# Three exact bf16 pieces for gathered tables and attention scores, block ends spread over more steps, and some products held back, in a four-layer graph network

## The chip, the cores and the metric

One core of a Trainium2 chip. The metric is device microseconds from the first to the last instruction of one execution. Every kernel below was run several times beside the kernel before on the same chip. Three chips were used for the experiments: one for e1 to e4, a second for e5 to e11, and a third for e12 to e14. On the first two the kernel before takes the same 2288 us; the third is slower, so its runs are kept apart.

## The reference, cut to what matters

There are 3327 nodes with 512 features and a sparse random adjacency matrix. Four layers follow each other, each with a residual and a layer norm. Layers 0 and 3 are graph attention (8 and 4 heads), layers 1 and 2 are means over neighbours.

```python
# layers 0 and 3
e    = leaky_relu(f_src[:, :, None] + f_dst[:, None, :])
attn = softmax(where(adj > 0, e, NEG_INF))
h    = elu(einsum('hnm,hmo->hno', attn, Wh))
# layer 1
agg = mask @ x / max(deg, 1)
out = relu(concat([x @ W_self + b_self, agg @ W_nb + b_nb]) @ W_comb + b_comb)
# layer 2: mean over the first 64 neighbours only
xj, xi = leaky_relu(nb_mean @ W_nb.T + b_nb), leaky_relu(X @ W_line.T + b_line)
# around each layer
x = layernorm(x + layer(x))
```

## The kernel before: the parts that matter

Rows are handled in 26 blocks of 128. The edges of a block come in chunks of 128. For each chunk POOL issues an indirect DMA (a gather) that fetches 128 table rows; DVE builds a 128 x 128 selection matrix; PE multiplies it with the rows and accumulates the block's sum. When a block's last chunk is done, a "block end" follows: residual, layer norm and the products that the next layer needs. The first seven blocks have 42 down to 10 chunks and are called heavy here; the other 19 have 9 down to 5, mostly 6 or 7, and are called light. "Moments" are a row's mean and variance, from which the layer norm is made.

Everything is written as generators. `Stages` advances each live one by one step per round, so a `yield` decides which instructions of other blocks come in between. In layers 1 to 3 each engine executes strictly in this program order; in layer 0 a scheduler chooses it.

```python
def step(self):
    for stages in list(self.live):
        if next(stages, self) is self:
            self.live.remove(stages)
...
def mean_group(item, table, near, gp, sp, pacc, accs, done):   # layers 1 and 2
    b, l, c0, g, at = item
    G = gather(gp, table, l, c0, g, D)                         # fp32 rows of 2 KB
    yield
    S = select(sp, ..., c0, g)
    yield
    for c in range(g):
        nc.tensor.matmul(accs[b], S[:, c, :], G[:, c, :], start=..., stop=...)
...
# attention scores (layers 0 and 3), fp32
nc.tensor.matmul(pe[:, c], ds[:, c*P:(c+1)*P], self.fall[:, H:, b], start=True, stop=True)
...
def summed(self, fin, acc, xb):          # block end of layers 0 and 3
    for s in range(2):                   # two halves of the heads
        nc.vector.tensor_scalar(rden[:, s], acc[s][..., OUT:OUT+1], 1e-30, None, ALU.max)
        nc.vector.reciprocal(rden[:, s], rden[:, s])
        nc.vector.tensor_mul(h[:, s], acc[s][..., :OUT], rden[:, s].to_broadcast(...))
    nc.vector.tensor_scalar(e, hq, 0.0, None, ALU.min)
    nc.scalar.activation(e, e, AF.Exp)
    nc.vector.scalar_tensor_tensor(hq, hq, 0.0, xb, ALU.max, ALU.add)
    yield
    nc.vector.tensor_add(e, e, hq)
    mv, rs = moments(fin, e)             # DVE statistics, then POOL computes rs = 1/std
    yield
    return e, mv, rs
...
def layer1_end(b, acc):
    yield
    ...                                  # y = relu(acc / deg + zb) + xb
    mv, rs = moments(fin, y)
    yield
    scaled(x2, y, mv, rs)                # DVE
    xt = transposed(fin, ps, x2)         # PE, then ACT
    yield
    nc.vector.tensor_add(tb, times(ps, xt, wn2), bn)
    store(t2_d, b, tb, 2)
    yield
    nc.vector.tensor_add(xi, times(ps, xt, wl2), bl)   # the "own" product
    nc.vector.scalar_tensor_tensor(xi, xi, SAGE_ALPHA, xi, ALU.mult, ALU.max)
    nc.vector.tensor_add(xres[b], xi, x2)
```

Of the kernel before, what the change touches and what calls it, by code (L numbers as in the profile page):

```python
# [8 lines left out]
F32 = mybir.dt.float32  # L9
# [522 lines left out]
GROUP = 4  # L532
SPAN = 10
RANGE = 60.0


class EdgeList:


    def __init__(self, pool, name, cuts, L, K, rounds, at):  # L540
        self.cuts, self.L, self.K, self.rounds, self.at = cuts, L, K, rounds, at
        self.idx = pool.tile([P, L], U32, name=f"idx{name}")
        self.dst = pool.tile([P, L], F32, name=f"dst{name}")
        self.near = None
        self.nmid = pool.tile([P, 1], F32, name=f"nmid{name}")
        self.reach = pool.tile([P, 1], F32, name=f"reach{name}")
# [33 lines left out]
def sparse_path(ctx, tc, flag_i, x, adj, l0_w, l0_a1, l0_a2, l1_w_self, l1_b_self, l1_w_nb, l1_b_nb,  # L580
# [42 lines left out]
    for l in lists[0]:  # L623
        l.near = keep.tile([P, l.L], F32, name="near" + l.idx.name)
    NL = sum(map(len, lists))
# [11 lines left out]

    def iota(name, n, dtype, step, base, mult):
        t = const.tile([P, n], dtype, name=name)
        nc.gpsimd.iota(t, pattern=[[step, n]], base=base, channel_multiplier=mult,  # L640
                       allow_small_or_imprecise_dtypes=True)
        return t
# [4 lines left out]
    nc.gpsimd.memset(ones, 1.0)  # L647
    code = iota("code", NP, U16, 1, 2, 0)
    place = iota("place", LMAX * P, I16, 1, 0, 0)
    lane1 = iota("lane1", P, F32, 1, 1, 0)  # L650
    slot = iota("slot", KMAX, F32, 1, 0, 0)
# [26 lines left out]
    t0_d = dram.tile([ROWS, H0 * (OUT0 + 2)], F32, name="t0_d")  # L678
    t1_d = dram.tile([ROWS, D], F32, name="t1_d")
    x1_d = dram.tile([NP, D], F32, name="x1_d")  # L680
    z1_d = dram.tile([NP, D], F32, name="z1_d")
    t2_d = dram.tile([ROWS, D], F32, name="t2_d")
    t3_d = dram.tile([ROWS, H3 * (OUT3 + 2)], F32, name="t3_d")
# [30 lines left out]
    def moments(fin, y):  # L714
        st = fin.tile([P, 6], F32, name="st")
        nc.vector.bn_stats(st, y)
        mv = fin.tile([P, 2], F32, name="mv")
        nc.vector.bn_aggr(mv, st)  # L718
        rs = fin.tile([P, 1], F32, name="rs")
        nc.gpsimd.tensor_scalar(rs, mv[:, 1:2], EPS, 1.0, ALU.add, ALU.mult)  # L720
        nc.gpsimd.tensor_tensor(rs, rs, mhalf, ALU.pow)
        return mv, rs

# [143 lines left out]

    def gather(pool, table, l, c0, g, width):
        t = pool.tile([P, GROUP, width], F32, name="gt")
        for c in range(g):  # L870
            nc.gpsimd.indirect_dma_start(  # L871
                out=t[:, c, :], out_offset=None, in_=table[:, :],
                in_offset=bass.IndirectOffsetOnAxis(ap=l.idx[:, c0 + c:c0 + c + 1], axis=0))
        return t

    def select(pool, which, c0, g):
        s = pool.tile([P, GROUP, P], F32, name="sel")
        nc.vector.tensor_tensor(s[:, :g, :], lane1[:, None, :].to_broadcast([P, g, P]),  # L878
                                which[:, c0:c0 + g, None].to_broadcast([P, g, P]), ALU.is_equal)
        return s  # L880


    class Gat:
        def __init__(self, name, table, H, OUT, w, wa, k):
            self.table, self.H, self.OUT, self.w, self.wa, self.k = table, H, OUT, w, wa, k
            self.M = OUT + 2
            self.fall = keep.tile([P, 3 * H, NB], F32, name=name + "fall")

        def products(self, ps, xt):
# [20 lines left out]
        def finish(self, pool, ps, pmean):  # L910
# [27 lines left out]
            nc.vector.tensor_sub(u, f1, sh)  # L938
            nc.vector.scalar_tensor_tensor(v, f1, GAT_ALPHA, sh, ALU.mult, ALU.subtract)
            sp = pool.tile([P, H], F32, name="sp")  # L940
            nc.vector.tensor_add(sp, bc[:, :H], bc[:, H:])
# [4 lines left out]
        def group(self, item, pools, accs, done):  # L946
# [5 lines left out]
            G = gather(gp, self.table, l, c0, g, H * M)  # L952
            ds = sp.tile([P, GROUP * P], F32, name="ds")
            nc.scalar.activation(ds[:, :g * P], place[:, c0 * P:(c0 + g) * P], AF.Abs, bias=l.nmid)  # L954
            yield
            S = select(sp, l.dst, c0, g)
            nc.vector.tensor_scalar(ds[:, :g * P], ds[:, :g * P], l.reach, None, ALU.is_lt)  # L957
            pe = pone.tile([P, GROUP, 2, H], F32, name="pe")
            for c in range(g):
                nc.tensor.matmul(pe[:, c], ds[:, c * P:(c + 1) * P], self.fall[:, H:, b], start=True, stop=True)  # L960
            yield
# [20 lines left out]
        def summed(self, fin, acc, xb):  # L982
# [5 lines left out]
            for s in range(2):  # L988
                nc.vector.tensor_scalar(rden[:, s], acc[s][:, :, OUT:OUT + 1], 1e-30, None, ALU.max)
                nc.vector.reciprocal(rden[:, s], rden[:, s])  # L990
                nc.vector.tensor_mul(h[:, s], acc[s][:, :, :OUT], rden[:, s].to_broadcast([P, hh, OUT]))  # L991
            hq = h.rearrange("p s h o -> p (s h o)")
            e = fin.tile([P, D], F32, name="e")
            nc.vector.tensor_scalar(e, hq, 0.0, None, ALU.min)
            nc.scalar.activation(e, e, AF.Exp)
            nc.vector.scalar_tensor_tensor(hq, hq, 0.0, xb, ALU.max, ALU.add)  # L996
            yield
            nc.vector.tensor_add(e, e, hq)
            mv, rs = moments(fin, e)
            yield  # L1000
# [17 lines left out]
    bias1 = wlay.tile([P, D], F32, name="bias1")  # L1018
    big = pool_in(lay, "l0big")
    mid = pool_in(lay, "l0mid")  # L1020
    work = Stages()
    with ExitStack() as pro:
# [30 lines left out]
        def fused_weights():  # L1053
# [19 lines left out]
            for k in range(2 * DC):  # L1073
                bb = wp.tile([P, P], F32, name="bb", bufs=2)
                nc.vector.tensor_copy(bb, bs[:, k].to_broadcast([P, P]))
                nc.tensor.matmul(pb, bb, wc[:, k, :], start=k == 0, stop=k == 2 * DC - 1)
            nc.vector.tensor_add(bias1, pb, bc)
            for r in range(2):
                nc.sync.dma_start(t1_d[r:r + 1, :], bias1[0:1, :])

# [32 lines left out]
    def layer0_end(b, acc):  # L1113
# [8 lines left out]
        nc.vector.tensor_add(tb, times(ps, xt, wn), bias1)  # L1122
        store(t1_d, b, tb, 2)
        yield
# [29 lines left out]
    def mean_group(item, table, near, gp, sp, pacc, accs, done):  # L1154
        b, l, c0, g, at = item
        G = gather(gp, table, l, c0, g, D)
        yield
        S = select(sp, l.near if near and l.near is not None else l.dst, c0, g)
        yield
        if at == 0:  # L1160
            accs[b] = pacc.tile([P, D], F32, name="acc")
        for c in range(g):
            nc.tensor.matmul(accs[b], S[:, c, :], G[:, c, :], start=at + c == 0, stop=at + c == chunks_of[b] - 1)  # L1163
        if at + g == chunks_of[b]:
# [3 lines left out]
    with ExitStack() as lay:  # L1168
# [6 lines left out]
        nc.sync.dma_start(bl, row(l2_b_line, D))  # L1175
        zero = wp.tile([1, D], F32, name="zero")
        nc.gpsimd.memset(zero, 0.0)
        for r in range(2):
            nc.sync.dma_start(t2_d[r:r + 1, :], zero)
        gp, sp = pool_in(lay, "l1g", 5), pool_in(lay, "l1s", 3)  # L1180
        fin = pool_in(lay, "l1f", 2)
        pacc, ps = pool_in(lay, "l1pa", 2, space=PSUM), pool_in(lay, "l1ps", 2, space=PSUM)

        def transposed_weights():
# [39 lines left out]
        def layer1_end(b, acc):  # L1224
            yield
            xb, zb = xin.pop(b)
            y = fin.tile([P, D], F32, name="e")
            nc.vector.scalar_tensor_tensor(y, acc, rdeg[:, b:b + 1], zb, ALU.mult, ALU.add)
            nc.vector.scalar_tensor_tensor(y, y, 0.0, xb, ALU.max, ALU.add)
            mv, rs = moments(fin, y)  # L1230
            yield
            x2 = fin.tile([P, D], F32, name="x2")
            scaled(x2, y, mv, rs)
            xt = transposed(fin, ps, x2)
            yield
            tb = fin.tile([P, D], F32, name="tb")
            nc.vector.tensor_add(tb, times(ps, xt, wn2), bn)  # L1237
            store(t2_d, b, tb, 2)
            yield

            xi = fin.tile([P, D], F32, name="xi")
            nc.vector.tensor_add(xi, times(ps, xt, wl2), bl)  # L1242
            nc.vector.scalar_tensor_tensor(xi, xi, SAGE_ALPHA, xi, ALU.mult, ALU.max)  # L1243
            nc.vector.tensor_add(xres[b], xi, x2)

# [4 lines left out]
        for item in groups():  # L1250
            b, at = item[0], item[4]
            if at == 0:
                xin[b] = [fin.tile([P, D], F32, name=n, bufs=3) for n in ("xb", "zb")]
                load(xin[b][0], x1_d, b)
                load(xin[b][1], z1_d, b)
            work.add(mean_group(item, t1_d, False, gp, sp, pacc, accs, layer1))
            work.step()
        work.drain()


    with ExitStack() as lay:
# [11 lines left out]
        def layer2_end(b, acc):  # L1273
            yield
            y = fin.tile([P, D], F32, name="e")
            nc.scalar.mul(y, acc, rnear if b == 0 else rdeg[:, b:b + 1])
            nc.vector.scalar_tensor_tensor(y, y, SAGE_ALPHA, y, ALU.mult, ALU.max)
            nc.vector.tensor_add(y, y, xres[b])
            mv, rs = moments(fin, y)
            yield  # L1280
            scaled(xres[b], y, mv, rs)
            xt = transposed(fin, ps, xres[b])
            yield
# [11 lines left out]
    with ExitStack() as lay:  # L1295
# [7 lines left out]
        def layer3_end(b, acc):  # L1303
            yield
            e, mv, rs = yield from g3.summed(fin, acc, xres[b])
            o = fin.tile([P, D], F32, name="o")
            scaled(o, e, mv, rs)
            store(out, b, o)
# [75 lines left out]
```

## Time and profile before

2298.68 us, median of three runs (2287.83 to 2299.12).

```profile
POOL rs L720 <- DVE mv L718: 80.4, 26, 7.0
DVE sc L964 <- PE pe L960: 26.7, 20, 2.4
DVE sc L964 <- DMA gt<-t_d,idx: 25.3, 19, 2.8
```

### The profile page before, as it was taken

What the parts mean: (1) busy time and instruction counts of PE and PEld (TensorE: products, weight loads), DVE (VectorE), ACT (ScalarE), POOL (GpSimd) and SP (SyncE); (2) the same over time, 40 slices, a digit from 0 to 9 for tenths busy, and PEclk for the clock granted to TensorE, in tenths of its full rate; (3) what the DMA queues carried; (4) which work ended last, traced back from release to release, by engine and by line L of the source; (5) the groups of instructions that cost most, each with busy time, mean ns of one, the idle gap of its engine ahead of it and who ended that gap; (6) DMA issues with size and microseconds to landing.
All of it is one profiled execution on the core that took longest, in us unless ns stands there. A gap on an engine that the chain in (4) does not pass through costs nothing.

```text
span 2293.5 us, 22330 instructions
## 1 busy us (share of the span) xinstructions
PE 1960.0 (85%) x6950; PEld 1182.5 (52%) x6950; DVE 1367.9 (60%) x3351; ACT 422.7 (18%) x1016; POOL 1095.7 (48%) x1251
## 2 busy tenths in 40 slices
PE   3999887889899998699788888789999978888785
PEld 1555576666566664344333333224444447766664
DVE  8954589888888773333333433213333347788897
ACT  2333233333332221000000000000111112212121
POOL 1000255443444441676454443477775547767563
PEclk9999888898899999799899989999999989988777
DMA  5343466676765653776454443377665547656553
GB/s 186 109 139 116 130 232 200 217 243 191 232 175 178 188 177 116 220 227 189 148 172 141 147 142 96 115 206 210 203 189 162 164 116 203 195 169 187 152 164 100
DMA packets 138902, 392.65 MB, mean 171 GB/s; under 512 B 27035, under 2 KB 28571, under 8 KB 138774
## 3 DMA queue, kind: packets, MB, share of 16 engines
q0 software_dynamic: 79040, 262.10, 39.6%
q1 hardware_dynamic: 59734, 129.03, 16.6%
q8 instruction: 58, 0.95, 0.2%
q14 instruction: 70, 0.57, 0.1%
HBM read 343.01 MB, written 48.03 MB: 170 GB/s over the span
## 4 chain that ended last, share of the span: by engine, by line
PE 38%; DVE 9%; DMA 5%; issue 4%; POOL 4%; ACT 1%; SPq 0%; POOLq 0%; DVEq 0%; ACTq 0%
PE acc L1163 16%; PE po L711 12%; PE acc L977 5%; DMA gt<-t_d,idx 4%; POOL gt L871 3%; PE pt L703 1%; PE pe L960 1%; PE pmean L907 1%; DVE h L991 1%; PE pf L893 1%; DVE xi L1243 1%; DVE xi L1242 1%; DVE h L996 1%; DVE x L725 1%; DVE gt L971 1%
## 5 line engine op out<-in xcount | busy, mean ns | idle before, releaser
L871 POOL DMA_INDIRECT gt<-t_d,idx x988 | 983.8, 996 | 600.4 <-issue 403.5
L977 PE MATMUL acc<-gt,sel 128*128 128x264 f32 (+1 forms) x1976 | 553.9, 436 | 81.2 <-issue 73.5
L1163 PE MATMUL acc<-gt,sel 128*128 128x512 f32 x988 | 493.8, 641 | 25.5 <-DMA gt<-t_d,idx 13.6
L977 PEld LDWEIGHTS acc<-gt,sel 128*128 128x128 f32 x1976 | 415.3, 217 | 175.6 <-issue 90.8
L1163 PEld LDWEIGHTS acc<-gt,sel 128*128 128x128 f32 x988 | 192.0, 205 | 267.7 <-issue 205.3
L971 DVE TENSOR_TENSOR gt<-gt,w 128x1536 f32<-128x1536 f32 (+2 forms) x148 | 284.7, 1923 | 1.5 <-ACT w L967 1.3
L878 DVE TENSOR_TENSOR sel<-lane,dst 128x384 f32<-128x384 f32 (+2 forms) x284 | 167.7, 592 | 70.3 <-PE acc L1163 37.4
L711 PE MATMUL po<-wn,xt 128*128 128x512 f32 x416 | 195.7, 612 | 5.6 <-ACT xt L705 5.2
L720 POOL TENSOR_SCALAR rs<-mv 128x1 f32<-128x1 f32 x104 | 29.8, 286 | 343.6 <-DVE mv L718 340.0
L711 PE MATMUL po<-w,xt 128*128 128x512 f32 x416 | 192.5, 604 | 1.5 <-ACT xt L705 1.5
L705 ACT COPY xt<-pt 128x512 f32<-128x512 f32 x112 | 65.7, 586 | 684.4 <-PE pt L703 684.4
L1237 DVE TENSOR_TENSOR tb<-po,bn 128x512 f32<-128x512 f32 x26 | 18.0, 692 | 204.6 <-PE po L711 204.6
L711 PEld LDWEIGHTS po<-w,xt 128*128 128x128 f32 x416 | 77.7, 192 | 105.5 <-issue 93.0
L711 PEld LDWEIGHTS po<-wn,xt 128*128 128x128 f32 x416 | 78.7, 195 | 96.4 <-issue 87.1
L954 ACT ACTIVATE ds<-place,nmid 128x384 f32<-128x384 int16 (+2 forms) x148 | 95.1, 644 | 163.0 <-PE pe L960 154.3
L779 DVE MAX8 cand<-val 128x8 f32<-128x832 uint16 (+39 forms) x259 | 124.3, 521 | 0.0
L695 POOL MEMSET xb<- 32x512 f32 x3 | 1.6, 519 | 229.5 <-PE pt L703 227.7
L703 PE MATMUL pt<-s_ident,x 128*128 128x128 f32 x208 | 38.1, 314 | 82.1 <-DVE x L725 70.8
L960 PE MATMUL pe<-g3fall,ds 128*128 128x8 f32 x494 | 64.8, 254 | 45.0 <-DVE ds L957 45.0
L711 PE MATMUL po<-wx,xt 128*128 128x512 f32 x208 | 97.1, 610 | 2.2 <-DVE tb L1122 1.8
L960 PEld LDWEIGHTS pe<-g3fall,ds 128*128 128x128 f32 x494 | 68.4, 201 | 58.1 <-issue 43.2
L967 ACT ACTIVATE w<-sc 128x24 f32<-128x24 f32 (+4 forms) x148 | 28.2, 191 | 380.0 <-DVE sc L965 267.7
(178 smaller groups left out, 2107.1 us busy)
## 6 DMA issues: line engine op xcount, KB each, us to landing
ab<-in_adj_dram SPq DMA_DIRECT2D x25, 832.0 KB, 6.5
ab<-in_adj_dram SPq DMA_DIRECT2D x25, 831.5 KB, 7.1
gt<-t_d,idx POOLq DMA_INDIRECT x988, 3.8
xb<-in_x_dram SPq DMA_DIRECT2D x50, 256.0 KB, 3.0
t_d<-tb SPq DMA_DIRECT2D x50, 256.0 KB, 2.2
t_d<-tg SPq DMA_DIRECT2D x25, 264.0 KB, 3.1
t_d<-tg SPq DMA_DIRECT2D x25, 260.0 KB, 3.8
x_d<-x SPq DMA_DIRECT2D x25, 256.0 KB, 2.8
```

The costliest lines, as they stand in the source:

```text
L703: nc.tensor.transpose(pt[:, c, :], src[:, c * P:(c + 1) * P], ident)
L705: nc.scalar.copy(xt, pt)
L711: nc.tensor.matmul(po, xt[:, c, :], w[:, c], start=c == 0, stop=c == DC - 1)
L720: nc.gpsimd.tensor_scalar(rs, mv[:, 1:2], EPS, 1.0, ALU.add, ALU.mult)
L779: nc.vector.max(out=top, in_=seg)
L871: nc.gpsimd.indirect_dma_start(out=t[:, c, :], out_offset=None, in_=table[:, :], in_offset=bass.IndirectOffsetOnAxis(ap=l.idx[:, c0 + c:c0 ...
L878: nc.vector.tensor_tensor(s[:, :g, :], lane1[:, None, :].to_broadcast([P, g, P]), which[:, c0:c0 + g, None].to_broadcast([P, g, P]), ALU.i ...
L954: nc.scalar.activation(ds[:, :g * P], place[:, c0 * P:(c0 + g) * P], AF.Abs, bias=l.nmid)
L960: nc.tensor.matmul(pe[:, c], ds[:, c * P:(c + 1) * P], self.fall[:, H:, b], start=True, stop=True)
L971: nc.vector.tensor_mul(Gc[:, :, :OUT], Gc[:, :, :OUT], w[:, :g].rearrange("p c (h o) -> p (c h) o", o=1).to_broadcast([P, g * H, OUT]))
L977: nc.tensor.matmul(accs[b][s], S[:, c, :], G[:, c, s * hh * M:(s + 1) * hh * M], start=at + c == 0, stop=at + c == chunks_of[b] - 1)
L1163: nc.tensor.matmul(accs[b], S[:, c, :], G[:, c, :], start=at + c == 0, stop=at + c == chunks_of[b] - 1)
```

## The change

Its intent is to relieve PE, to stop waits that bind block ends of neighbouring blocks together, and to take work off DVE. A sum of three bf16 numbers holds an fp32 value exactly, and the selection matrix holds only zeros and ones, so one fp32 product may become three bf16 products. The core of the diff:

```diff
-    t1_d = dram.tile([ROWS, D], F32, name="t1_d")          # and t2_d
+    t1_d = dram.tile([ROWS, 3 * D], BF16, name="t1_d")
+    def pieces(t3, t):
+        nc.scalar.copy(t3[:, 0], t)
+        yield
+        nc.vector.tensor_sub(t, t, t3[:, 0])
+        yield
+        nc.scalar.copy(t3[:, 1], t)
+        yield
+        nc.vector.tensor_sub(t3[:, 2], t, t3[:, 1])
@@ mean_group
-            nc.tensor.matmul(accs[b], S[:, c, :], G[:, c, :], ...)
+            for k in range(3):
+                nc.tensor.matmul(accs[b], S[:, c, :], G[:, c, k * D:(k + 1) * D], ...)
@@ scores (layers 0 and 3)
-                nc.tensor.matmul(pe[:, c], ds[...], self.fall[:, H:, b], start=True, stop=True)
+                for k in range(3):
+                    nc.tensor.matmul(pe[:, c], ds[...], self.own[:, k, :, b], start=k == 0, stop=k == 2)
@@ summed (layers 0 and 3)
-                nc.vector.reciprocal(rden[:, s], rden[:, s])
+            nc.vector.reciprocal(rden, rden)
-            nc.vector.tensor_scalar(e, hq, 0.0, None, ALU.min)
-            nc.scalar.activation(e, e, AF.Exp)
+            nc.scalar.activation(e, hq, AF.Exp)
+            yield
             nc.vector.scalar_tensor_tensor(hq, hq, 0.0, xb, ALU.max, ALU.add)
-            yield
-            nc.vector.tensor_add(e, e, hq)
-            mv, rs = moments(fin, e)
+            nc.vector.scalar_tensor_tensor(e, e, 1.0, hq, ALU.min, ALU.add)
+            mv = moments(fin, e)
+            yield
+            rs = rstd(fin, mv)
             yield
@@ layer0_end: the table for layer 1 is stored in pieces
+        for _ in pieces(t3, tb): pass
@@ layer1_end
-            mv, rs = moments(fin, y)
-            yield
-            scaled(x2, y, mv, rs)
-            xt = transposed(fin, ps, x2)
+            mv = moments(fin, y)
+            yield
+            rs = rstd(fin, mv)
+            yield
+            scaled(x2, y, mv, rs)
+            yield
+            xt = transposed(xts, ps, x2)
+            yield
+            po = times(ps, xt, wn2)
             yield
-            nc.vector.tensor_add(tb, times(ps, xt, wn2), bn)
-            ...                                        # own product follows here
+            nc.vector.tensor_add(tb, po, bn)
+            own = own_part(b, xt)                      # the own product, now its own stage
+            if b < NB - LATE: work.add(own)            # LATE = 4: the last four are held back
+            else: late.append(own)
+            yield from pieces(t3, tb)
@@ last scaling of layer 3
-            scaled(o, e, mv, rs)                       # DVE
+            nc.vector.scalar_tensor_tensor(nm, mv[:, 0:1], -1.0, rs, ALU.mult, ALU.mult)
+            nc.scalar.activation(o, e, AF.Identity, bias=nm, scale=rs)
```

Cut away: the selection matrices' inputs in bf16, residual rows loaded straight into their place, steps added in layer 2's block end, four buffers for gathered rows in layer 1 instead of five, and the drain loop that starts the products held back.

## The prediction

> **What bounds the kernel now.** I read the page first, then busy time by stretch, then the timeline of single blocks, then the groups by shape. The clock is fast (granted 0.92 over the span), so there is no slow state to allow for. The program is four layers in turn. Layer 0, which also builds the edge lists, ends at about 905 us. Layer 1 runs to 1462, layer 2 to 1884, layer 3 to 2294. Each layer walks 26 blocks of 128 rows, and the edges of a block come in chunks of 128: by the tables in the code 42, 19, 15, 13, 11, 10, 10, 9, 9, 8, 8, then 7 five times, 6 eight times, 5 twice, 247 in all. So "x988" gathers are 247 in each of four layers, and the 988 records of a mean layer's product are two records for each of 2 x 247 fp32 products. Busy time by stretch (PE, weight load, DVE, ACT, POOL, clock, DMA share, GB/s):
>
> ```profile
> 250.00:905.00 655.00, 577.47 (x2508) 418.06 (x2507) 528.01 (x1290) 199.83 (x512) 277.89 (x303) 0.91 0.62 193
> 935.00:1100.00 165.00, 148.27 (x340) 65.07 (x341) 62.67 (x115) 3.51 (x6) 107.55 (x117) 0.94 0.64 195
> 1100.00:1462.00 362.00, 298.52 (x675) 131.39 (x674) 132.56 (x226) 11.70 (x20) 152.26 (x170) 0.91 0.44 134
> 1462.00:1600.00 138.00, 123.77 (x290) 47.64 (x291) 29.94 (x66) 8.02 (x13) 105.88 (x114) 0.98 0.71 206
> 1600.00:1836.00 236.00, 236.00 (x711) 108.10 (x710) 84.30 (x221) 34.62 (x59) 156.22 (x180) 1.00 0.61 180
> 2090.00:2294.00 204.00, 151.19 (x590) 122.52 (x590) 170.30 (x362) 36.13 (x108) 107.53 (x126) 0.78 0.49 144
> ```
>
> The reader is to see four different limits. Layer 0 is DVE's (528 of 655 us). The light blocks of layer 2 are wholly PE's (236 of 236). Its heavy first blocks are the gather's: 106 gathers in 138 us, each about 0.95 us busy and 0.30 us of issue, 1.26 us start to start. Layer 3 is DVE's. Layer 1 is nobody's: PE 298 of 362 at clock 0.91, DVE and POOL less than half. Its timeline says why:
>
> ```profile
> 1365.77 1.45 PE L711 MATMUL po<-wl,xt 128*128 128x512 f32 x3
> 1367.26 0.69 DVE L1242 TENSOR_TENSOR xi<-po,bl 128x512 f32<-128x512 f32 x1 [2.54 <-PE po L711]
> 1369.32 0.54 DVE L725 TENSOR_SCALAR x<-e,mv,rs 128x512 f32<-128x512 f32 x1
> 1370.01 0.88 PE L703 MATMUL pt<-s_ident,x 128*128 128x128 f32 x4 [2.79 <-DVE x L725]
> 1370.68 4.22 PE L1163 MATMUL acc<-gt,sel 128*128 128x512 f32 x6
> 1374.74 3.60 PE L711 MATMUL po<-wn,xt 128*128 128x512 f32 x8
> ```
>
> DVE, in order, waits for the previous block's own product (wl) to finish before it can scale this block's row; PE then idles until that is done. After the gap the next six records take 4.22 us instead of 2.7: PE also came back at half speed. The same transpose-to-transpose period is about 17 us per light block.
>
> **What the Trainium skill says.** "FP8 and Floating Point Precision", section "TensorE Precision Notes": true fp32 takes four passes of the array. This trace agrees: in the chain of waits eight records (four products of 512 columns) take 3.43 us, 858 ns each, four passes of 214 ns. "TensorE: Matmul & The Clock Gate", section "Wait — 56ns, not 53.3ns?": a warm 512-column matmul starts every 215.7 ns; a quarter of the measured 858 agrees. Same page, "HAM oscillation — how this bites in real kernels": an idle gap over about 3.4 us sends PE back to half clock. Agrees: weight loads idle 3.58 us, then records at 0.85 us instead of 0.43. "DMA: Bandwidth & Descriptors", section "Bandwidth": 341 GB/s for a 1 MB load and about 358 as a core's share of memory. Here 206 GB/s goes with a share of 0.71, so these 2 KB-row gathers would saturate near 290; direct loads in layer 0 come to some 320.
>
> **The change, part by part.**
>
> *Mean products (layers 1, 2).* One fp32 product (858 ns) becomes three bf16 products, 3 x 215 = 645 ns, with 3 weight loads. No bf16 load is in this trace; the fp32 one lasts 190 ns and hides behind a 214 ns pass, so I take the new ones as hidden. Saved: 0.213 x 247 = 53 us of PE per mean layer. In exchange a gathered row is 3 KB instead of 2, 393 KB a chunk. At 290 GB/s that is 1.36 us of DMA, above the 1.26 us that POOL needs. If part of a row's cost is fixed, a longer row is cheaper per byte (estimate 1.2 us). I take 300 GB/s, 1.31 us.
>
> *Block ends a step apart (layer 1 above all).* Scaling moves away from the wait on wl, and rs is issued a step after its moments. A light block then costs PE 6 x 0.645 + 2 x 3.43 (wn, wl) + 0.42 (transposes) = 11.2 us, POOL 6 x 1.26 + 1.3 (rs) = 8.9, DVE about 8.1 (with pieces), DMA 6 x 393 KB + 0.9 MB (two loads, one store) = 3.26 MB, 10.9 us at 300 GB/s. So 17 becomes 11.2 to 12: the largest single gain. Whole layer: 7 heaviest blocks, 120 chunks, 53.5 MB, 180 us on DMA (POOL alone 160); 19 others, 127 chunks, PE 82 + 19 x 7.28 = 220 us (DMA 67 MB, 224), 235 with friction; start and tail 30. Sum 445 against 527 from 935 to 1462: **-82 us**. In it: the products held back fill PE while the last row waits for its store; the two last blocks' serial tail (1430 to 1462) becomes about 20 us.
>
> *Layer 2.* PE was already full, and no gap is removed. Per light block 11.02 us (measured) falls by 6 x 0.213 to 9.7; DMA 6 x 393 + 266 KB is 8.7 and POOL 8.9. But now the gather is longer than PE (0.645 x chunks + 5.8) for all blocks of 8 chunks or more: 11 blocks, 154 chunks, 63.5 MB, 212 us. The other 15: PE 60 + 87 = 147, say 152. Sum 364 against 374 (1462 to 1836): **-10 us**. The 53 us of saved PE time are mostly lost to the gather.
>
> *Pieces.* Per block two ACT copies (0.585 each) and two DVE subtractions (0.69 each), 26 blocks. In layer 1 DVE and ACT have room. In layer 0 DVE is the bound: +26 x 1.38 = 36 us.
>
> *Summed (layers 0 and 3).* Gone from DVE: the minimum (0.43) and one pair of reciprocals (one of 0.17, since two become one): 26 x 0.60 = 15.6 us per layer. The exp now reads h directly. Layer 0: +36 - 16 = +20 on DVE, 0.8 of it seen, plus 2 us for a longer last store: **+18 us**.
>
> *Layer 3's last scaling* goes from DVE (0.60) to ACT, with a tiny DVE product (0.15): -0.45 x 26. With the 15.6 above DVE loses about 27 us. A light block there holds 11.1 us of DVE work in an 11.0 to 12.3 us period, so it shows; in the three heaviest blocks (76 chunks), which go at the gather's pace, it doesn't: **-20 us**.
>
> *Scores.* Two records of about 0.12 us in a burst per chunk (eight pe records in 0.96 us) become three small bf16 ones with three loads: no gain or loss I can size, 0. The bf16 selectors: inner operand broadcast, so I expect the same 0.55 us; 0.
>
> Sum: 18 - 82 - 10 - 20 = -94 us, 2299 to 2205. I lean a little lower, **2195 us**, since layer 1's gap removal may also spare clock elsewhere, and 3 KB rows may be cheaper per byte than I took.
>
> **Rivals.** (1) *The gather takes over wholly.* 3 KB rows at 290 GB/s or worse, or a row costing POOL two descriptors. For it: share 0.71 x 1.5 = 1.07 in layer 2's heavy blocks. Against: POOL's 0.95 us goes with 128 rows, not with bytes (2112-byte rows of layer 0 and 2048-byte rows cost the same). If DMA saturates at 280 the two layers lose about 30 us against my sum: 2225. If POOL doubled to some 2.2 us, each mean layer takes 540 us and the kernel gets slower, about 2420; I give that 3%. (2) *DMA rows get cheaper with length.* Then heavy blocks go at POOL's 1.26 us and light ones at PE's pace: layer 1 at 415, layer 2 at 350, total near 2150. (3) *Layer 1's gap turns into another wait*: DVE waiting for ACT's bf16 copy, or rs standing in POOL's queue behind a gather that waits for a buffer (4 instead of 5). The order of the changed program puts a step between each pair, so I expect little; if half the gap stays, 2240. (4) *Layer 0 gets off free or pays double*: its order is set by a scheduler, so +0 to +35.
>
> **Range and chances.** 8 in 10: 2125 to 2250. The lower end is rival 2 with layer 0 free, the upper rival 1 or 3 with a full bill in layer 0. Faster by over 2% needs under 2253: 0.89. Within 2%: 0.09. Slower: 0.02. Most of this rests on layer 1's gap, which is plainly seen 23 times.
>
> **What would show it.** Right: mean products at three records in about 0.65 us; light blocks of layer 1 at 11 to 12.5 us with no PE wait for DVE's scaling and no half-speed records; heavy blocks of both mean layers with DMA share over 0.9 and gathers 1.26 to 1.4 us apart; layer 2 almost as long as before; layer 0 longer by 10 to 25 us. Wrong: gather instructions of POOL clearly over 1 us on average; weight loads showing between bf16 passes (three products over 0.75 us); layer 2 shorter by over 30 us (gather cheaper than I think); layer 0 not longer.

## More of the kernel before

The four layers are easiest to compare if cut at the first gather of each. The next view is busy time by stretch of the kernel before; its columns are the stretch, its length, the busy time (and count) of PE, weight load, DVE, ACT and POOL, then the granted clock, the DMA share and GB/s.

```profile
0.00:907.66 907.66, 787.65 (x3351) 533.24 (x3352) 699.76 (x1997) 273.40 (x654) 285.38 (x324) 0.94 0.56 176
907.66:1458.88 551.22, 454.49 (x1047) 201.64 (x1045) 193.35 (x339) 20.29 (x35) 274.37 (x302) 0.91 0.53 160
1458.88:1861.15 402.27, 379.81 (x1069) 165.17 (x1069) 126.46 (x331) 47.98 (x81) 266.11 (x299) 0.99 0.61 179
1861.15:2293.50 432.35, 338.03 (x1484) 282.41 (x1484) 348.30 (x686) 81.05 (x246) 269.89 (x327) 0.84 0.59 169
```

One row per layer. The reader should notice two rows that the prediction didn't weigh enough: layer 0's PE (787.65) is busier than its DVE (699.76), and PE is idle for 22% of layer 3, which also has the lowest granted clock of the four, 0.84. The waits in this section are those in layer 3 (engine, line, releaser: us in total, times, longest).

In each of the 26 block ends POOL stands before `rs` until DVE's moments are done, 3.1 us on average. Of the 80.4 us, 62.2 fall where gathers still stand behind it in POOL's queue; the last few blocks have none. DVE itself waits 26.7 us for score products and 25.3 us for gathered rows.

## The result, and the profile after

| kernel | median us | runs | range us |
|---|---|---|---|
| before | 2297.59 | 4 | 2287.83 to 2299.12 |
| changed | 2111.15 | 4 | 2103.77 to 2116.49 |

Ratio 0.9195, 95% interval 0.9156 to 0.9233. (A ratio here is the mean time of one kernel's fast runs over that of the other's of the same rounds, so not quite the ratio of the medians.) The kernel is 8% faster. The direction was predicted; the time, 2195 us with a range from 2125 to 2250, was not: it fell below the range.

Busy time of the changed kernel by layer, the same columns as above:

```profile
0.00:904.03 904.03, 765.43 (x3598) 502.46 (x3598) 719.35 (x2002) 306.15 (x711) 290.69 (x324) 0.93 0.56 180
904.03:1344.73 440.70, 378.78 (x1293) 171.88 (x1294) 226.19 (x395) 50.36 (x86) 272.78 (x301) 0.94 0.81 282
1344.73:1731.46 386.73, 334.13 (x1316) 150.36 (x1315) 122.84 (x320) 47.68 (x82) 265.78 (x299) 0.97 0.80 270
1731.46:2108.50 377.04, 274.82 (x1731) 222.44 (x1731) 315.36 (x644) 103.70 (x274) 268.81 (x327) 0.91 0.67 194
```

| layer | before | changed | difference | predicted |
|---|---|---|---|---|
| 0 | 907.7 | 904.0 | -3.6 | +18 |
| 1 | 551.2 | 440.7 | -110.5 | -82 |
| 2 | 402.3 | 386.7 | -15.5 | -10 |
| 3 | 432.3 | 377.0 | -55.3 | -20 |

Layer lengths come from one profile per kernel. In all kernels of the experiments' table but e3 layer 2 is computed alike; there it took 384.3 to 387.7 us, so I read differences of more than about 4 us. In layer 0 the DVE time rose by 20 us, exactly as predicted, and yet the layer didn't grow, while PE's time fell by 22 us. e1 tests whether the one explains the other.

A light block of layer 1 in the changed kernel, from its timeline (start, length, engine, line, operation; the bracket is idle time before it and what ended it):

```profile
1198.58 0.54 DVE L738 TENSOR_SCALAR xres<-e,mv,rs 128x512 f32<-128x512 f32 x1
1199.02 3.60 PE L711 MATMUL po<-wl,xt 128*128 128x512 f32 x8
1202.46 3.60 PE L711 MATMUL po<-wn,xt 128*128 128x512 f32 x8
1202.66 0.69 DVE L1291 TENSOR_TENSOR xi<-po,bl 128x512 f32<-128x512 f32 x1 [3.54 <-PE po L711]
1205.89 2.11 PE L1193 MATMUL acc<-gt,sel 128*128 128x512 bf16 x9
1207.83 0.60 PE L703 MATMUL pt<-s_ident,xres 128*128 128x128 f32 x4
1208.27 2.10 PE L1193 MATMUL acc<-gt,sel 128*128 128x512 bf16 x9
```

DVE still waits 3.54 us for wl, but now the scaling (1198.58) was done ahead of that wait, and PE goes from one product to the next. Nine bf16 records, the products of three chunks, take 2.10 us. Light blocks follow each other at 11.2 us, where before it was 17.1. The heavy blocks (980 to 1097), the light ones, the tail of layer 1 and the heavy start of layer 2, in the changed kernel by stretch:

```profile
980.00:1097.00 117.00, 95.28 (x343) 41.40 (x343) 45.61 (x79) 9.60 (x16) 87.94 (x96) 0.97 0.91 318
1097.00:1315.00 218.00, 215.56 (x735) 100.40 (x733) 139.97 (x242) 31.30 (x54) 136.95 (x157) 0.99 0.82 287
1315.00:1344.73 29.73, 23.43 (x54) 10.12 (x53) 16.79 (x27) 4.78 (x8) 0.74 (x2) 0.94 0.14 53
1345.00:1485.00 140.00, 102.56 (x378) 40.10 (x378) 29.71 (x62) 6.66 (x11) 107.16 (x116) 0.94 0.89 304
```

PE fills the light stretch (215.56 of 218). In layer 2's heavy stretch DMA is at 0.89 and PE has 37 of 140 us free: the gather took over, as predicted.

And layer 3's waits after, to hold against the above:

```profile
DVE sc L983 <- DMA gt<-t_d,idx: 24.8, 16, 3.5
DVE sc L983 <- PE pe L978: 11.2, 8, 2.9
POOL rs L723 <- DVE mv L718: 8.4, 4, 3.4
```

The view puts only 8.4 us of POOL's waits before `rs` down to the moments, and others to other tiles: all of them together are 24.0 us, of which 6.3 have gathers behind them. Before, they were 80.4 and 62.2.

### The profile page after: what moved, and what is told of

Its sections match the earlier page's. It is cut to its first block, busy times and chain, and to the rows that moved or that the text cites. A ratio compares the mean times of both kernels' runs of the same rounds, so it can differ in the third digit from the quotient of the medians.

```text
span 2108.5 us, 24358 instructions
## 1 busy us (share of the span) xinstructions
PE 1753.2 (83%) x7938; PEld 1047.1 (50%) x7938; DVE 1383.7 (66%) x3358; ACT 507.9 (24%) x1152; POOL 1098.1 (52%) x1251
## 3 DMA queue, kind: packets, MB, share of 16 engines
q1 hardware_dynamic: 59734, 135.85, 18.2%
## 4 chain that ended last, share of the span: by engine, by line
PE 55%; POOL 13%; DVE 13%; issue 11%; DMA 5%; ACT 1%; SPq 0%; POOLq 0%; DVEq 0%; ACTq 0%
PE po L711 23%; PE acc L996 15%; POOL gt L884 13%; PE acc L1193 6%; DMA gt<-t_d,idx 5%; PE pv L845 3%; DVE gt L990 3%; PE pt L703 2%; PE pmean L921 2%; PE pf L907 2%; DVE cand L792 1%; PE pe L978 1%; DVE sel L891 1%; DVE st L716 1%; DVE h L1011 1%
## 5 line engine op out<-in xcount | busy, mean ns | idle before, releaser
L996 PE MATMUL acc<-gt,sel 128*128 128x264 f32 (+1 forms) x1976 | 528.6, 422 | 133.5 <-issue 115.4
L996 PEld LDWEIGHTS acc<-gt,sel 128*128 128x128 f32 x1976 | 400.1, 209 | 223.4 <-issue 135.0
L1193 PE MATMUL acc<-gt,sel 128*128 128x512 bf16 x1482 | 374.6, 391 | 89.0 <-DMA gt<-t_d,idx 75.3
L1193 PEld LDWEIGHTS <-sel 128*128 128x128 bf16 x1482 | 146.5, 101 | 298.3 <-issue 146.2
L891 DVE TENSOR_TENSOR sel<-lane,dst 128x384 f32<-128x384 bf16 (+4 forms) x284 | 167.0, 592 | 80.6 <-PE acc L1193 50.8
L970 ACT ACTIVATE far<-place,nmid 128x384 f32<-128x384 int16 (+2 forms) x148 | 94.7, 642 | 57.9 <-DVE ds L974 44.2
L729 ACT CAST t<-tb 128x512 bf16<-128x512 f32 x52 | 32.1, 617 | 278.6 <-DVE tb L1275 199.6
L711 PE MATMUL po<-wl,xt 128*128 128x512 f32 x208 | 94.2, 597 | 0.0
L762 ACT ACTIVATE m<-ab 128x1664 bf16<-128x1664 int32 x52 | 82.5, 1586 | 34.4 <-DVE val L772 22.2
L978 PEld LDWEIGHTS <-ds 128*128 128x128 bf16 x1482 | 60.2, 98 | 54.6 <-DVE ds L974 34.4
```

Of the source, the lines that this page charges most:

```text
L711: nc.tensor.matmul(po, xt[:, c, :], w[:, c], start=c == 0, stop=c == DC - 1)
L762: nc.scalar.activation(m, ab[s], AF.Sign, accum_out=half[:, s, b:b + 1])
L891: nc.vector.tensor_tensor(s[:, :g, :], lane1[:, None, :].to_broadcast([P, g, P]), which[:, c0:c0 + g, None].to_broadcast([P, g, P]), ALU.i ...
L970: nc.scalar.activation(far[:, :g * P], place[:, c0 * P:(c0 + g) * P], AF.Abs, bias=l.nmid)
L978: nc.tensor.matmul(pe[:, c], ds[:, c * P:(c + 1) * P], self.own[:, k, :, b], start=k == 0, stop=k == 2)
L996: nc.tensor.matmul(accs[b][s], S[:, c, :], G[:, c, s * hh * M:(s + 1) * hh * M], start=at + c == 0, stop=at + c == chunks_of[b] - 1)
```

## The experiments

Each run of this table is the changed kernel with one or two parts undone, timed over three rounds (e12 to e14 follow below); lengths of layers are from the profile of a fast run. All outputs are right.

| run | L0 | L1 | L2 | L3 | median us | ratio to before |
|---|---|---|---|---|---|---|
| changed | 904.0 | 440.7 | 386.7 | 377.0 | 2111.15 | 0.9195 |
| e1 fp32 scores | 926.5 | 440.5 | 387.0 | 377.5 | 2131.25 | 0.9301 |
| e2 old block ends in 0 and 3 | 902.2 | 439.6 | 385.8 | 419.5 | 2147.81 | 0.937 |
| e3 fp32 tables | 888.3 | 456.2 | 408.2 | 372.9 | 2126.7 | 0.9281 |
| e4 old block ends in 1 | 905.3 | 548.7 | 387.6 | 375.8 | 2219.23 | 0.9684 |
| e5 new operations, old steps | 900.5 | 441.6 | 385.8 | 414.6 | 2143.65 | 0.9354 |
| e6 old operations, new steps | 914.6 | 440.1 | 387.7 | 403.6 | 2146.22 | 0.9366 |
| e7 nothing held back | 907.4 | 435.5 | 384.3 | 376.4 | 2108.88 | 0.9211 |
| e8 held ones after the last store | 904.6 | 439.3 | 385.3 | 373.7 | 2111.25 | 0.9222 |
| e9 old ends and fp32 scores | 924.5 | 438.1 | 386.0 | 426.8 | 2173.32 | 0.9499 |
| e10 1/std at once | 911.1 | 441.3 | 386.6 | 393.2 | 2134.66 | 0.9314 |
| e11 maximum early | 906.1 | 440.5 | 386.2 | 399.6 | 2133.54 | 0.9316 |

### e1: the scores alone

```diff
-                for k in range(3):
-                    nc.tensor.matmul(pe[:, c], ds[...], self.own[:, k, :, b], start=k == 0, stop=k == 2)
+                nc.tensor.matmul(pe[:, c], ds[...], self.fall[:, H:, b], start=True, stop=True)   # fp32
```

> The changed kernel with its score products in fp32 again (one product of two records a chunk, no pieces of the scores). Theory A (the bf16 scores are what shortened layer 3 by 55 us and kept layer 0 from growing): about +40 us, 2150, layer 3 some 400 us long. Theory B (layer 3 gained from the cheaper block ends on DVE and from their spreading over two steps): under +8 us, 2111 to 2119.

Neither theory's numbers held: A was right on layer 0 and wrong on layer 3. Layer 0 took 926.5 us, 22.5 more; layer 3 the same. This is the piece that the prediction set to 0. Groups of PE's score products between 300 and 900 us, first of the changed kernel, then of e1 (line, engine, operation, tile, size, count, busy us and mean ns):

```profile
L978 PE MATMUL pe<-g0own,ds 128*128 128x16 bf16 x699 | 32.5, 192 | 1.3 <-DVE ds L974 1.0 <-DVE sl L810 0.3
```

```profile
L975 PE MATMUL pe<-g0fall,ds 128*128 128x16 f32 x472 | 59.1, 255 | 1.6 <-DVE ds L972 1.2 <-DVE sc L980 0.4
```

Three bf16 records for two fp32 ones, and yet 26.6 us less PE time. For small products the mean of one record says little, since they overlap; the busy sum tells it. Between e1 and the changed kernel DVE's busy time in layer 0 is the same (718 and 719 us) and PE's is not (799 and 765), so it is PE's time that reached the layer's length. In layer 3 fp32 scores do make DVE wait longer for scores, 22.2 us instead of 11.2, but it then waits less for gathered rows, 13.4 instead of 24.8: the sum is the same, and so is the layer.

### e2: the old block ends of layers 0 and 3

`summed` and the last scaling as they were before.

```diff
-            nc.scalar.activation(e, hq, AF.Exp); yield; max+add; min+add; moments; yield; rstd; yield
+            min; nc.scalar.activation(e, e, AF.Exp); max+add; yield; add; moments; rstd; yield
-            nm = ...; nc.scalar.activation(o, e, AF.Identity, bias=nm, scale=rs)
+            scaled(o, e, mv, rs)
```

> The changed kernel with the block ends of layers 0 and 3 as before (minimum ahead of the exp, two reciprocals, rs in the same step, last scaling on DVE). Theory B: layer 3 longer by 35 to 50 us with its granted clock back near 0.80 in the light blocks, total about 2155. Theory B' (only the removed DVE time counts, 27 us a layer 3): +20 to +27, about 2135, clock unchanged. Theory A: under +15.

Layer 3 took 419.5 us: these block ends are worth 42.5 us there, and nothing in layer 0 (902.2), although DVE's busy time there rose from 719 to 729 us. The DVE time removed in layer 3 is 347.3 - 315.4 = 32 us, less than the gain, so something else is in it. e5, e6, e10 and e11 look for it. The layer's granted clock went from 0.91 back to 0.86 as well. It moves along with the length in all these runs (0.84 before, 0.86 in e5 and e11, 0.87 in e6, 0.89 in e10); what the clock itself adds to a difference was not separated.

### e3: the tables alone

Tables, gathers and selections in fp32 and one product per chunk; all else new.

```diff
-    t1_d = dram.tile([ROWS, 3 * D], BF16)                    # and t2_d; no pieces() anywhere for them
+    t1_d = dram.tile([ROWS, D], F32)
-            for k in range(3):
-                nc.tensor.matmul(accs[b], S[:, c, :], G[:, c, k * D:(k + 1) * D], ...)
+            nc.tensor.matmul(accs[b], S[:, c, :], G[:, c, :], ...)
```

> The changed kernel with fp32 tables of 2 KB rows and one fp32 product a chunk in layers 1 and 2. Theory C (my prediction's sums: PE-bound light blocks lose 6 x 0.213 us each, heavy blocks are the gather's either way): layer 1 +15 to +25, layer 2 +15, layer 0 -5 for the missing pieces, total about 2140. Rival D (the bf16 pieces are most of the gain of the two layers): +60 or more, 2170.

Layer 0 fell by 15.7 us (its block ends no longer make pieces), three times what was expected; the run takes ACT's two copies and the longer stores out with DVE's subtractions, and can't tell them apart. Layer 1 rose by 15.5, layer 2 by 21.5. A light block of layer 1 takes 12.5 us instead of 11.2 and of layer 2 11.0 instead of 9.7, which is the six chunks' 6 x 0.213 us of the prediction. Net, tables in pieces are worth 15 to 21 us, about as much as the scores (20 us in e1) and much less than the block ends.

### e4: the old block ends of layer 1

```diff
+            mv = moments(fin, y); rs = rstd(fin, mv)
+            yield
+            scaled(x2, y, mv, rs); xt = transposed(xts, ps, x2)
+            yield
+            add(tb, times(ps, xt, wn2), bn); pieces; store
+            yield
+            add(xi, times(ps, xt, wl2), bl) ...             # nothing held back
```

> The changed kernel with layer 1's block ends in the old order (scaling and transposes in one step, rs with its moments, own product a step after the first, nothing held back), bf16 tables kept. Gap theory: light blocks of layer 1 go from 11.2 back to 15 or more us with PE waiting for DVE's scaling and half-speed records; layer 1 longer by 70 to 110 us, total 2180 to 2220. Rival D: under +30.

Layer 1 went back to 548.7 us, so 108 of its 110.5 us depend on the order. Set beside e3, the parts do not add: with the old order the pieces are worth 2.5 us in layer 1 (551.2 against 548.7), with the new order 15.5. Light blocks took 16.6 us, and the granted clock of the layer fell to 0.88. PE's largest wait in this layer of e4, and none in the changed kernel's:

```profile
PE pt L703 <- DVE xres L738: 83.7, 24, 4.5
```

This is the gap theory's wait, the transposes for DVE's scaling; in the kernel before it was 70.3 us. POOL's waits for the moments come back too (166.8 us in layer 1 against 47.3). The run undoes four things at once (the pause between scaling and transposes, that between moments and 1/std, the order of the two products, the holding back), and how the 108 us divide among the first three was not measured; e7 shows that the fourth brings nothing. The 2.5 us are below what one pair of profiles resolves.

### e5 and e6: operations without steps, steps without operations

```diff
 # e5: the new operations in the old steps
             nc.scalar.activation(e, hq, AF.Exp)
-            yield
             nc.vector.scalar_tensor_tensor(hq, hq, 0.0, xb, ALU.max, ALU.add)
+            yield
             nc.vector.scalar_tensor_tensor(e, e, 1.0, hq, ALU.min, ALU.add)
             mv = moments(fin, e)
-            yield
             rs = rstd(fin, mv)
             yield
 # e6: the old operations (and the scaling on DVE) with the new yields
```

> The changed kernel with its cheaper block-end operations of layers 0 and 3 (no minimum, one reciprocal, last scaling on ACT) but in the old steps (the maximum ahead of the first pause, rs right after its moments, one pause fewer). In the runs so far the old block ends cost 42.5 us in layer 3 (419.5 against 377.0) of which 32 us is DVE time. Theory B1 (the DVE time removed is what counts): layer 3 stays within 12 us of the changed kernel, 377 to 389, total 2111 to 2123. Theory B2 (spreading the ends over more steps is what counts): layer 3 at 400 or more, total 2134 or more.

> The changed kernel with the old operations of the block ends (minimum, two reciprocals, last scaling on DVE) in the new steps. B1: layer 3 about 405 to 412, total about 2140. B2: layer 3 at 395 or less, total under 2129.

Layer 3: 414.6 and 403.6 us. From e2's 419.5 the operations alone bring 4.9, the steps alone 15.9, both together 42.5. Neither theory's numbers held for both runs: each said that one half would carry most of it. The clue was in the waits of e5 in layer 3:

```profile
POOL rs L723 <- DVE mv L718: 49.5, 23, 5.7
DVE sc L983 <- DMA gt<-t_d,idx: 40.1, 22, 4.1
DVE h L1015 <- ACT e L1014: 18.2, 26, 0.8
```

The third line is new, and exists neither before nor in the changed kernel at this size: DVE's maximum waits for ACT's exponential, 26 times, 0.7 us each. The exponential now reads `hq` itself rather than a copy with the minimum taken, and the maximum overwrites `hq` in place. Issued straight behind the exponential, it must wait for it to have read.

### e9, e10, e11: one step at a time

```diff
 # e10: 1/std in the step of the moments         # e11: maximum ahead of the pause
             mv = moments(fin, e)                 +            max+add on hq
-            yield                                             yield
             rs = rstd(fin, mv)                   -            max+add on hq
```

e9 is e2 with e1's fp32 scores as well.

> The changed kernel with both the old block ends of layers 0 and 3 and the fp32 score products. With the old block ends alone layer 3 took 419.5 us, against 432.3 in the kernel before; with fp32 scores alone 377.5, as in the changed kernel (377.0). Theory S: the missing 13 us are the scores, which are worth something in layer 3 only while the block ends are old, because DVE then waits for the score products. Then layer 3 is 429 to 435 and the kernel about 2182. Rival R: they are the rest of the change (selectors in bf16, the held own products): then layer 3 stays at 417 to 423, and the kernel at about 2169 (the scores cost 22.5 in layer 0 in either case).

> The changed kernel with POOL's 1/std of layers 0 and 3 issued in the same step as the DVE moments it reads, all else new. With all the old steps layer 3 took 414.6 against 377.0. Theory P: it is this step: POOL, in order, waits for the moments with the gathers behind it. Then layer 3 is over 405 here. Rival M: it is the maximum before the pause (the exponential's wait), then layer 3 stays under 385 here.

> The changed kernel with the maximum-and-add of layers 0 and 3 issued before the pause rather than after it; the 1/std keeps its own step. Theory P (POOL's wait for the moments is what the steps take away): layer 3 stays at 375 to 385. Rival M (DVE's place of the maximum counts): over 395.

e10 (393.2) fell between theory and rival; e11 (399.6) fell in the rival's range, but e10 does not agree with that rival. Both steps count. Put in a table, layer 3 comes apart cleanly:

| layer 3, us | 1/std at once | 1/std a step later | gain of the step |
|---|---|---|---|
| old operations | 419.5 (e2) | 403.6 (e6) | 15.9 |
| new operations, maximum early | 414.6 (e5) | 399.6 (e11) | 15.0 |
| new operations, maximum after the pause | 393.2 (e10) | 377.0 (changed) | 16.2 |

So the step between moments and 1/std is worth 15 to 16 us whatever else is done. The new operations are worth 26 us (419.5 to 393.2, 403.6 to 377.0), but only 4 to 5 us, hardly above what is resolved, if the maximum stays early. The 21 to 23 us lost then are mostly the wait on the exponential, which is itself 18.2 us in e5 and 19.0 in e11. What looked like an interaction of two halves was one operation that needs its step. (e6 also moved the maximum, but its exponential read a copy, so that there was nothing to wait for.) e10's and e11's waits in layer 3 agree, first e10, then e11:

```profile
DVE sc L983 <- DMA gt<-t_d,idx: 38.4, 25, 4.3
POOL rs L723 <- DVE mv L718: 30.9, 20, 5.7
```

```profile
POOL rs L723 <- DVE mv L718: 29.6, 16, 3.4
DVE sc L983 <- DMA gt<-t_d,idx: 20.5, 16, 2.1
DVE h L1015 <- ACT e L1014: 19.0, 26, 0.8
```

In e10 the wait of `rs` comes back and with it 13.6 us more of DVE waiting for gathered rows (38.4 against 24.8): POOL's wait delays the gathers behind it. The other two pairs agree: with the step, DVE's wait for rows in layer 3 falls from 31.6 to 17.3 us (e2 to e6) and from 40.1 to 20.5 (e5 to e11). That POOL waits 29.6 us in e11 too, without DVE getting its rows later, suggests that such a wait counts only where it holds back a gather that someone soon needs.

e9's layer 3 took 426.8, between the 429 to 435 of the theory and the 417 to 423 of the rival: with old ends the fp32 scores cost 7.3 us there. The theory's reason shows too: DVE waits 27.1 us for scores in e9 and 11.1 in e2, and gets back part of it at the rows (21.7 against 31.6). The last 5.5 us up to the 432.3 of before stay open.

### e7 and e8: the products held back

```diff
 # e7
-            if b < NB - LATE:
+            if b < NB:
 # e8: in the drain loop
-            if late and len(late) + len(work.live) < LATE + 2:
-                work.add(late.pop(0))
```

> The changed kernel with no product held back: each block's own product follows a step after its other product, up to the last block. The changed kernel's layer 1 has 30.1 us from its last block's moments to layer 2's first gather, the kernel with fp32 tables (same holding back) 18.5. Intent of the change (the held-back products fill gaps and shorten the tail): layer 1 longer by 5 to 12 us. Rival (their DVE additions stand in front of the last row's pieces, DVE being in order): layer 1 shorter by 0 to 6 us. Other layers unchanged within 3 us.

> The changed kernel with the held-back products moved behind the last row's store: none is started while other stages still run. If the additions of the held-back products stand in front of the last pieces: the tail falls from 30.1 to about 24 us and the kernel gains 4 to 7 us, about 2105, since layer 2 starts with a gather-bound block that hides the late PE work. If not: tail unchanged, or the first product of layer 2 as much later as the gather is earlier, 2111 or slightly more.

Layer 1 took 435.5 us without holding back: holding back costs about 5 us there rather than helping, as e7's rival said. The end of layer 1 in the changed kernel:

```profile
1337.40 0.68 DVE L731 TENSOR_TENSOR tb<-tb,t 128x512 f32<-128x512 f32 x1
1338.16 0.69 DVE L1291 TENSOR_TENSOR xi<-po,bl 128x512 f32<-128x512 f32 x1
1338.89 0.69 DVE L1292 SCALAR_TENSOR_TENSOR xi<-xi 128x512 f32<-128x512 f32 x1
1339.62 0.69 DVE L1293 TENSOR_TENSOR xres<-xi,xres 128x512 f32<-128x512 f32 x1
1340.23 0.68 DVE L735 TENSOR_TENSOR t<-tb,t 128x512 bf16<-128x512 f32 x1
1344.73 1.09 POOL L884 DMA_INDIRECT gt<-t_d,idx  x1 [28.01 <-DMA t_d<-t]
```

Layer 2's first gather waits for the last row's store, and the last subtraction for that store (L735) stands behind three additions of a held product, which were meant only to fill. e8 takes these additions away, and its own trace shows what comes instead:

```profile
1332.22 0.69 DVE L735 TENSOR_TENSOR t<-tb,t 128x512 bf16<-128x512 f32 x1 [0.68 <-ACT t L733]
1343.88 1.00 POOL L884 DMA_INDIRECT gt<-t_d,idx  x1 [26.44 <-PE po L711]
```

The last subtraction is 8 us earlier, so the additions did delay the store. But layer 2's first gather now waits for the last of the held products on PE instead, and comes hardly sooner. From the start of the last row's statistics to that gather it takes 29.8 us in the changed kernel, 28.3 in e8 and 24.5 in e7. So e8's expected 4 to 7 us did not come: the held products cost time on either side of the store. On the whole kernel the difference isn't resolved: 2108.88 (ratio 0.9211, e7) and 2111.25 (0.9222, e8) against 2111.15 (0.9195).

### e12, e13, e14: layer 0's pieces on POOL

A try at a better kernel: e7 with layer 0's two piece subtractions per block end moved from DVE to POOL.

```diff
-        for _ in pieces(t3, tb): pass
+        for _ in pieces(t3, tb, nc.gpsimd): pass      # both tensor_sub on POOL
```

> A try at a better kernel: nothing held back in layer 1 (that alone gave 2108.9, layer 1 at 435.5), and the two piece subtractions of each of layer 0's block ends on POOL instead of DVE (1.38 us of DVE in each of 26 ends). The fp32 tables had shown that these pieces cost layer 0 15.7 us. If that is DVE's time, layer 0 falls from 904 to 890 to 897 and the kernel to 2093 to 2103; rival: it is the longer chain of the block end, or POOL's gathers are held behind the subtractions, then layer 0 stays at 900 or more, and the kernel at 2105 to 2125.

It fell on another chip, where the kernel before took 2403.35 us instead of 2288 and the granted clock of the whole kernel was lower (0.90 here, against 0.936). Its 2259.32 us (ratio 0.9457) can't be set beside the others. So it was run again, beside e7's kernel on that same chip:

> Nothing held back in layer 1, pieces on DVE: the reference for the next run on the same chip. On a chip like the first ones: layer 0 902 to 908, layer 1 434 to 438, kernel 2100 to 2112.

> The same with layer 0's piece subtractions on POOL. If the pieces cost DVE's time: layer 0 10 to 16 us shorter than in the run beside it. If they cost the length of the block end (two subtractions of 1.2 us on POOL against 0.69 on DVE) or POOL's gathers: layer 0 the same or up to 15 us longer. The other layers the same within 2 us if the clock is the same.

e13, pieces on DVE: 2258.0 us (ratio 0.9429), layer 0 918.4. e14, pieces on POOL: 2258.29 us (0.9447), layer 0 917.4. The same. (e13's kernel is e7's, which took 2108.88 us. Most of the difference of the chips lies in layer 3, 460.7 us here and 376.4 there, with DVE equally busy, the granted clock 0.83 against 0.92, and DVE waiting 75.3 us for something that the profile only calls "remote"; in layer 0 the clock was the same, 0.92. This was not followed up. So the size of the gain, 7.9% there and 5.7% here, was not the same on all chips.) DVE lost 52 instructions of 0.69 us, which is 36 us, but its busy time in layer 0 fell only from 719.75 to 708.89. Two groups of DVE from 271 to 917 us, of e13 and then of e14:

```profile
L891 DVE TENSOR_TENSOR sel<-lane,dst 128x384 f32<-128x384 bf16 (+1 forms) x74 | 44.2, 598 | 31.0 <-PE acc L996 30.8
L974 DVE TENSOR_SCALAR ds<-far,reach 128x384 bf16<-128x384 f32 (+1 forms) x74 | 33.2, 448 | 0.0
```

```profile
L892 DVE TENSOR_TENSOR sel<-lane,dst 128x384 f32<-128x384 bf16 (+1 forms) x74 | 50.6, 683 | 26.4 <-PE acc L997 25.7 <-issue 0.4
L975 DVE TENSOR_SCALAR ds<-far,reach 128x384 bf16<-128x384 f32 (+1 forms) x74 | 39.8, 538 | 0.0
```

DVE's own instructions became longer, 598 to 683 and 448 to 538 ns, while POOL's subtractions took 1194 ns each. In blocks of 384 columns `sel` took 949 ns where it overlapped one of them and 551 elsewhere, `ds` 1198 and 410. These two groups are 13 of the 25 us that DVE didn't save. For `sel`, which reads two tensors, this agrees with the Trainium skill, "SBUF — State Buffer", section "SBUF: two separate sides": a DVE operation with two SBUF inputs and a POOL operation that reads SBUF shut each other out for a whole instruction. `ds` has one tensor input; the page counts such an operation only in a two-port mode, and no run here shows in which mode `ds` ran. Work moved to POOL wasn't free to DVE. None of the kernels run beats the changed one by a difference that these runs resolve.

## Why the prediction was wrong, point by point

The mechanisms of layers 1 and 2 were right; the sum (-94 us) was half of the truth (-185 between the two profiles). Of the 91 us missed, 35 lie in layer 3, 28 in layer 1, 22 in layer 0 and 5.5 in layer 2.

*Layer 3, predicted -20, measured -55.3: the largest miss.* The step that failed is the paragraph on layer 3's last scaling, "With the 15.6 above DVE loses about 27 us", of which -20 was counted: it priced the block ends only by the DVE time they remove. It held that "A light block there holds 11.1 us of DVE work in an 11.0 to 12.3 us period", so that DVE is full. That sum counts overlapping instructions twice: added up they last 11.2 us, but DVE is busy for only 10.5 of the 12.06 us of a light block. Over the layer DVE was idle for 77.0 us before and for 53.9 after, and in these waits lay the rest of the gain. The DVE time itself was roughly right (26 us realised, e2 against e10). Left out were the step between moments and 1/std, 16 us by e2 against e6 and by e10 against the changed kernel, and the scores, 7.3 us while the ends are old (e9). The wait of POOL for the moments, 80.4 us, could be read in the view before; rival 3 names only its reverse, `rs` standing behind a gather, and only in layer 1. 5.5 us stay open.

*Layer 1, predicted -82, measured -110.5.* The mechanism was right to the tenth: light blocks at 11.2 us, and e4 shows that the order carries 108 us. What was mis-sized is "Sum 445 against 527 from 935 to 1462". From the first gather on, the changed layer takes about 193 us through its seven heavy blocks, 218 for the light ones and 30 of tail. The prediction gave the heavy ones 180 from 935, on top of the 27 us from first gather to 935 that it let stand; it gave the light ones 235 "with friction", of which there was none (PE 215.56 of 218 us). Long rows helped less than rival 2 had it: the heavy stretch ran at 318 GB/s, share 0.91, with a gather every 1.41 us where that rival had POOL's 1.26. No run asks why that is slower than layer 2's 1.31.

*Layer 0, predicted +18, measured -3.6.* One term failed outright: the scores, set to "0", were worth -22.5 us (e1). The pieces cost 15.7 us (e3), half of the 31 that the prediction's own terms give for them (0.8 of 36, and 2 for the store). That even this is DVE time was not shown: cheaper ends that save DVE 10 us leave the layer's length (e2), and moving the subtractions to POOL leaves it too (e14, in which DVE's busy time fell by only 11 us). "Layer 0 not longer" stood among the prediction's own signs of being wrong, and it came. The reading behind both, "Layer 0 is DVE's", overlooked that PE was busier there (577 against 528 us in the very line that it rests on). -22.5 + 15.7, with nothing for the ends, is -6.8, near the measured -3.6; e2's 902.2 against 904.0 shows the scatter.

*Layer 2, predicted -10, measured -15.5: right.* Light blocks at 9.7 us as worked out, and the heavy ones left PE waiting for the gather. Without it the pieces would have saved all of 53 us of PE; they saved 21.5 (e3). Why the layer as a whole gained 6 us less was not followed up; its tail, from the start of the last row's statistics to layer 3's first gather, grew from 14.5 to 21.2 us, which is the size of it. The added steps may be the reason; no run tests it.

*Rivals.* (1), POOL doubling, did not come: a gather's mean stays 996 ns in both mean layers. (2) is partly right: longer rows are cheaper per byte (206 GB/s at share 0.71 is 290 at a full share before; 304 at 0.89 is 342 after), but the pace of layer 2's heavy blocks, some 107 gathers in 140 us, is 1.31 us, what the prediction took. (3) did not come: waits of DVE for wl remain, but block nothing. (4) came as "off free", for another reason than the scheduler.

## What to carry to other kernels

Price a reordering by the queue behind the wait, not by the work it removes: a small operation on an in-order engine that waits for another engine holds back all that stands behind it, and in layer 3 one extra step was worth 16 us with no work removed. When an operation is made cheaper by reading a buffer directly instead of a copy, look for who overwrites that buffer next, for the wait on the reader can take back the whole gain. And when two undone halves don't add up, split by single steps and lay the runs out as a table: what looks like an interaction may be one dependence.

## What the Trainium skill lacked or had wrong

- "TensorE: Matmul & The Clock Gate", section "Back-to-back issue gap", gives a sustained 131 ns per 512-column matmul in a stream with weight loads, and 216 ns as the isolated gap. Here nine bf16 records, each with its own weight load, take 2.10 us; with 0.38 us for a record's own length that is (2.10 - 0.38) / 8 = 215 ns. The 216 holds, the 131 was not seen.
- "FP8 and Floating Point Precision", section "TensorE Precision Notes", has the four passes of fp32 but not the cost of a small one, nor that three bf16 pieces with a 0/1 operand stand in exactly: 32.5 against 59.1 us of PE for the same 16-column scores, and 0.65 against 0.86 us for 512 columns.
- "DMA: Bandwidth & Descriptors", section "Why small descriptors are slow (HBM only)", has joining descriptors into packets as worth it only up to 256 bytes a descriptor. Gathered rows of 3 KB moved at about 342 GB/s per full share against 290 for 2 KB, and no section has the pace of gathers: POOL's own 1.26 us for 128 rows, whatever their length.
- No page that I read says how far two chips may differ: the kernel before took 2288 us on two of them and 2403 on a third. One and the same kernel (e7, e13) spent 376 us in layer 3 on one and 461 on the other, at granted clocks of 0.92 and 0.83, though both had the same clock in layer 0.
